# A delta-rule layer's last round with values ahead of queries, MLP weights over the masked operands, and the MLP norm's weight on the transposed input

## The chip, the cores and the metric

The kernel runs on one core of one Trainium2 chip. The metric is the device time of a run in microseconds (us); of several runs the median is given. Engines are named as in the profile: PE (TensorE matmuls), PEld (its weight loads), DVE (VectorE), ACT (ScalarE), POOL (GpSimd) and SP (SyncE, whose queue issues most of the DMAs). "L823" is line 823 of the kernel.

## The reference

The input is `x` (128 sequences of 32 tokens, 512 channels, fp32) and a context of 257 tokens per sequence. Three residual layers follow one another, each on a layer norm of `x`: a cross-attention, a delta-rule layer with its own SwiGLU MLP, and a Hadamard-rotated quantised feed-forward. The change lies in the second one:

```python
h = _rms(x, attn_norm_w)
q = silu(silu(_causal_dwconv(h @ Wq.T, conv_q)))     # 4 taps along the 32 tokens
k = silu(silu(_causal_dwconv(h @ Wk.T, conv_k)))
v = silu(silu(_causal_dwconv(h @ Wv.T, conv_v)))
q, k = _l2norm(q), _l2norm(k)                        # per head: 32 heads of 16
beta = jax.nn.sigmoid(h @ Wbeta.T)
o, memory_state = _delta_scan(k, q, v, beta)         # S -= beta * (S k - v) k^T ; o = S q
o = _rms(o, out_norm_w) @ Wout.T
x = x + o
h2 = _rms(x, mlp_norm_w)
x = x + silu(h2 @ Wgate.T) * (h2 @ Wup.T) @ Wdown.T  # 512 -> 1408 -> 512
```

The two norm weights `out_norm_w` and `mlp_norm_w` multiply channels, so they can be put on the rows of the weight matrices that read the normed tensor, or on the tensor itself.

## The kernel before

The program is written for a scheduler that keeps each engine's instructions in one fixed order and adds the semaphores; pools give the tiles their addresses, and a tile placed over the address of an earlier one waits for that one's last reader. Four stages follow each other: `cross_attention` (0 to about 697 us in the profile), `delta_products` (to about 1236), `delta_out_mlp` (to about 2413) and `hadamard_ffn` (to the end).

`delta_products` takes the 4096 tokens in 8 groups (rounds) of 512. A round has twelve channel steps: for each of four chunks of 128 channels a key step and a query step, k, q, k, q and so on, and then four value steps. A step is four 128x512 matmuls (L520, 3.44 us together), the convolution's taps and the activations. From keys and queries come two things: squared lengths (`add`, L577 to L581, then `lengths` and `by_tokens`), and, a block of 128 tokens at a time, the products of keys with keys and queries (`products`, L455 to L462), for which SP makes masked copies of `kq` (`kqm`, loaded at L550). The products go to DRAM as `ld` and `pd`. `put_v` (L618 to L627) transposes a finished value chunk on PE, scales it on DVE (L621, into `vt`) and stores it from POOL (L627, into `vd`). The reciprocal query lengths are stored by POOL too (L609, `rq`). In the last round the products of the last group are not made in the phase: keys and queries are stored as they are (`kd`, L666, on SP's queue), and `late_products` in the next phase makes them from there.

`delta_out_mlp` takes the tokens in 16 blocks of 256. For each block `back(b)` builds the outputs: it loads the solved `u` (L743), POOL spreads it into `um` (L750), SP loads `pe` (L757) from `pd`, PE multiplies them (L764), DVE makes `oT` (L777) with the lengths `r` (L773); then comes the output projection with `wo` (L797), the residual `y` (L800), the MLP norm's factor (L807, L808, L811), a transpose of each 128-token tile on PE (L97) and the copy of its result into `hT` (L812), one ACT instruction per tile. `mlp(b)` runs the gate (`wg`, L823) and up (`wu`, L826) matmuls on `hT`, silu on ACT (L828), the product `mT` on DVE (L829), the down projection (`wd`, L834) in two halves of 128 tokens, the residual add `xo` on DVE (L839), and then the next layer's statistics (L81, L82), `z` (L844) and butterflies (L126, L127). Beside it run `late_products` (masked loads `km`, L856, and `k`, L858) and the substitution solver, whose DVE steps (L432, L436, L442) get shorter from 31 x 64 to 1 x 64 elements per group of tokens. The function `mixed` interleaves these lists by given costs, and the last group's solve ends at about 2150 us.

At the border of the two phases the weights are loaded on SP's queue, in the trace in this order: `wo` and the first half of `wg` (L103), the MLP norm's weight `mnw` (L874), the first half of `wu`, the second halves, and after the first part of `back(0)` `wd`. DVE scales `wo` by the output norm, and ACT, at L888, `wg` and `wu` by `mnw` (sixteen instructions). In memory `wg` lies over masked operands and `wu` over masked operands and `kq`; the tile of `mnw` lies over `wv`.

Of the kernel before, what the change touches and what calls it, by code (L numbers as in the profile page):

```python
# [26 lines left out]
H = 32  # L27
HD = 16
TAPS = 4
SG = 512  # L30
EARLY = 24
FF = 1408
FC = FF // P
# [13 lines left out]
def pools(tc, *specs):  # L47


    stack = ExitStack()  # L50
    got = []
    for name, bufs, *space in specs:
        kw = {"space": space[0]} if space else {}
        got.append(stack.enter_context(tc.tile_pool(name=name, bufs=bufs, reuse_waits="tile", **kw)))
    return stack, got
# [44 lines left out]

def load_rows(nc, dst, src):

    nc.sync.dma_start(dst, src.rearrange("(c p) n -> p c n", p=P))  # L103


def mixed(*steps):


    lists = [[0.0, total, s] for total, s in steps if s is not None]
    while lists:  # L110
        one = min(lists, key=lambda a: a[0] / a[1])
        cost = next(one[2], None)
        if cost is None:
            lists.remove(one)
        else:
            one[0] += cost
# [268 lines left out]
NG = NT // SG  # L385
# [79 lines left out]
def delta_products(  # L465
# [8 lines left out]
    tc, nc = g.tc, g.nc  # L474
    KT = 256

    stack, (xp, wp1, hp, wk1, wp, st, wk, wp2, wk2, wp3, wk3, psn, psp, ps, psg) = pools(
        tc, ("b_x", 3), ("b_w1", 1), ("b_hn", 2), ("b_h", 2), ("b_w", 1), ("b_st", 2), ("b_k", 2),
        ("b_w2", 1), ("b_v", 2), ("b_m", 4), ("b_g", 6), ("b_pn", 1, PSUM), ("b_pp", 3, PSUM),
        ("b_ps", 2, PSUM), ("b_pg", 2, PSUM),  # L480
    )
    with stack:
        w, cw = {}, {}
        for n, src, p in (("k", wkT, wp1), ("q", wqT, wp1), ("v", wvT, wp2)):
            w[n] = p.tile([P, DC, D], FP, name=f"w{n}")
            load_rows(nc, w[n], src)
        w["b"] = wp.tile([P, DC, H], FP, name="wb")
# [7 lines left out]
        nc.sync.dma_start(cm, causal)  # L495
        scaled_rows(nc, wp, "nw", norm_w, [w["k"], w["q"], w["v"], w["b"]])

        kqm = [wp3.tile([P, HH, 2, KT], FP, name=f"kqm{i}", bufs=1) for i in range(3)]
        blank = [t[:, h] for t in kqm for h in range(HH)]
        mv, rs = stats  # L500

# [64 lines left out]
        class Group:  # L566
# [13 lines left out]
                nc.tensor.matmul(self.sums[H : 2 * H], w["b"][:, ec, :], hT[:, ec, :], **at)  # L580
                nc.tensor.matmul(self.sums[2 * H :], hs[:, ec, :], sq[:, 1], **at)  # L581

            def lengths(self):

                f = self.factors = wk.tile([3 * H, SG], FP, name="f", bufs=1)
                nc.scalar.activation(f[H : 2 * H], self.sums[H : 2 * H], AF.Tanh, scale=0.5)
                for r in (slice(0, H), slice(2 * H, 3 * H)):
                    nc.scalar.activation(f[r], self.sums[r], AF.Sqrt)

            def by_tokens(self):  # L590
                f = self.factors
                pt = ps.tile([P, GT, 2 * H], FP, name="ps")
                for i in range(GT):
                    nc.tensor.transpose(
                        pt[:, i, :], f[0 : 2 * H, i * P : (i + 1) * P], g.ident[0 : 2 * H, 0 : 2 * H]
                    )
                self.n = st.tile([P, GT, H], FP, name="n")
                nc.vector.tensor_scalar_max(self.n, pt[:, :, 0:H], 1e-12)
                self.beta = st.tile([P, GT, H], FP, name="beta")
                nc.vector.tensor_scalar(self.beta, pt[:, :, H:], 0.5, 0.5, ALU.mult, ALU.add)  # L600
                n2 = st.tile([P, GT, H], FP, name="n2", bufs=1)
                nc.vector.tensor_mul(n2, self.n, self.n)
                nc.vector.reciprocal(n2, n2)
                nc.vector.tensor_mul(self.beta, self.beta, n2)
                q = f[2 * H :]
                nc.vector.tensor_scalar_max(q, q, 1e-12)
                nc.vector.reciprocal(q, q)
                for c in range(DC):
                    nc.gpsimd.dma_start(  # L609
                        rq[self.gi, :, :, c].rearrange("i h t -> h i t"),  # L610
                        f[2 * H + c * HH : 2 * H + (c + 1) * HH].rearrange("h (i t) -> h i t", t=P),
                    )
# [25 lines left out]
        def a_round(gi, old, hT, made):  # L638
            new = Group(gi)
            made.append(new)  # L640
            xt, kq = [], {}
            if gi + 1 < NG:
                hT_next = wk1.tile([P, DC, SG], FP, name="hT")
                made.append(hT_next)
            for j, (n, ec) in enumerate(todo):
                if n == "v":
                    dst = new.v[ec] = wk2.tile([P, SG], FP, name="v2", bufs=4)
                else:
                    if n == "k":
                        kq[ec] = wp3.tile([P, 2, SG], FP, name="kq")  # L650
                    dst = kq[ec][:, "kq".index(n)]
                acc, last = channels(hT, n, ec)
                with tc.issue_after(last):
                    for _ in range(min(HH, len(blank))):
                        nc.vector.memset(blank.pop(0), 0.0)

                for _ in range(tiles[j]):
                    if count["done"] < per * len(held) and (old or j >= 4):
                        multiply()
                activated(acc, dst)  # L660
                if n == "q":
                    if gi < NG - 1:
                        pieces.extend((gi, ec, half, kq[ec]) for half in range(SG // KT))
                        hold()
                    else:
                        nc.sync.dma_start(kd[:, ec], kq[ec])  # L666
                if 3 <= j <= 9 and j % 2:
                    new.add(kq[(j - 3) // 2], hT, (j - 3) // 2)
                if j in loads and gi + 1 < NG:
                    xt.append(load((gi + 1) * GT + len(xt)))  # L670
                if j == 9:
                    new.lengths()
                    if gi == 0:
                        g.factors(*(t[:, EARLY:] for t in stats))
                if j == 11:
                    new.by_tokens()
                if j >= 8 and gi + 1 < NG:
                    normed((gi + 1) * GT + j - 8, xt[j - 8], hT_next)
                if old and j < DC:
                    old.put_v(j)  # L680
                yield 1
            if gi + 1 == NG:
                for ec in range(DC):
                    new.put_v(ec)

        hT = wk1.tile([P, DC, SG], FP, name="hT")
        for i in range(GT):
            normed(i, load(i), hT)
        old = None
        for gi in range(NG):  # L690
            made = []
            mixed((len(todo), a_round(gi, old, hT, made)), *beside(gi))
            old, hT = made[0], made[-1]
        assert count["done"] == per * len(pieces)


def delta_out_mlp(
# [14 lines left out]
    with stack:  # L712
# [4 lines left out]
        for t in (*um, *pe, km):  # L717
            nc.gpsimd.memset(t, 0.0)
        cm = lp.tile([P, T], FP, name="cm")
        wo = wp.tile([P, DC, D], FP, name="wo")  # L720
        wg = wp.tile([P, DC, FF], FP, name="wg")
        wu = wp.tile([P, DC, FF], FP, name="wu")
        wd = wp.tile([P, FC, D], FP, name="wd")
        inv_d = st.tile([P, 1], FP, name="inv_d", bufs=1)
        nc.vector.memset(inv_d, 1.0 / D)
        turn = {"pe": 0, "um": 0}
# [6 lines left out]
        def back(b):  # L733
# [75 lines left out]
            hT = wk2.tile([P, DC, TB], FP, name="hT")  # L809
            for i in range(NTL):  # L810
                nc.vector.tensor_scalar_mul(ys[i], ys[i], r[:, i : i + 1])  # L811
                nc.scalar.copy(hT[:, :, i * P : (i + 1) * P], g.transposed(ps, ys[i], g.ident))  # L812
                yield 2
            ready[b] = hT, xs

# [59 lines left out]

        for cols in (slice(0, 6 * P), slice(6 * P, FF)):
            for t, src in ((wg, wgT), (wu, wuT)):
                load_rows(nc, t[:, :, cols], src[:, cols])
        nc.sync.dma_start(cm, causal)
        mark = []  # L880
        first, late = back(0), late_products()
        mixed((4.0, part(first, 4.0)), (1.0, part(late, 1.0)))
        scaled_rows(nc, st, "onw", onorm_w, [wo])
        load_rows(nc, wd, wdT)
        for cols in (slice(0, 6 * P), slice(6 * P, FF)):
            for t in (wg, wu):
                for dc in range(DC):
                    nc.scalar.mul(t[:, dc, cols], t[:, dc, cols], nw[:, dc : dc + 1])  # L888
        mixed((12.0, first), (3.0, part(late, 3.0)))
        for b in range(NBL):  # L890
            mixed(
# [282 lines left out]
```

## Time and profile before

| what | value |
|---|---|
| time, median of 3 runs | 3081.3 us (3078.63 to 3082.94) |
| the profiled execution's own time | 3082.62 us |
| its span in the trace | 3080.8 us |
| mean granted PE clock | 0.986 |
| PE busy | 2924.4 us (95%) |
| PEld busy | 1678.8 us (54%) |
| DVE busy | 2077.8 us (67%) |
| ACT busy | 1040.3 us (34%) |
| POOL busy | 650.6 us (21%) |
| last value matmul of the last round ends | 1223.8 us |
| first gate matmul of the MLP | 1283.74 us |

Busy times come from the page's first part, the two moments from the timeline of PE. A row of the profile's groups reads: line, engine, operation, output<-input, number of instructions, then busy us, mean ns of one, and the idle time of the engine just before them with what ended it. A row of a timeline reads: start, us, engine, line, operation, count. In the page's rows of 40 digits each digit is one fortieth of the span (77 us).

### The profile page before, as it was taken

What the parts mean: (1) busy time and instruction counts of PE and PEld (TensorE: products, weight loads), DVE (VectorE), ACT (ScalarE), POOL (GpSimd) and SP (SyncE); (2) the same over time, 40 slices, a digit from 0 to 9 for tenths busy, and PEclk for the clock granted to TensorE, in tenths of its full rate; (3) what the DMA queues carried; (4) which work ended last, traced back from release to release, by engine and by line L of the source; (5) the groups of instructions that cost most, each with busy time, mean ns of one, the idle gap of its engine ahead of it and who ended that gap; (6) DMA issues with size and microseconds to landing.
All of it is one profiled execution on the core that took longest, in us unless ns stands there. A gap on an engine that the chain in (4) does not pass through costs nothing.

```text
span 3080.8 us, 42042 instructions
## 1 busy us (share of the span) xinstructions
PE 2924.4 (95%) x15558; PEld 1678.8 (54%) x15558; DVE 2077.8 (67%) x3557; ACT 1040.3 (34%) x1716; POOL 650.6 (21%) x963
## 2 busy tenths in 40 slices
PE   8999999999999999699999999999999899999998
PEld 3444443433333333467666766677777466666665
DVE  2353534336699797368778787878322599999997
ACT  1111111216666666212212121121111255555554
POOL 1121212113686664321211111001000000000000
PEclk9999999999999999799999999999999999999999
DMA  9798989763554544642322313131310111111110
GB/s 330 264 308 276 314 298 324 262 214 110 158 152 131 173 127 153 168 126 62 124 89 89 108 55 112 48 107 53 130 47 37 52 37 40 42 42 42 41 33 21
DMA packets 258235, 408.08 MB, mean 132 GB/s; under 512 B 68336, under 2 KB 170864, under 8 KB 254576
## 3 DMA queue, kind: packets, MB, share of 16 engines
q1 hardware_dynamic: 223856, 305.21, 31.8%
q0 software_dynamic: 34176, 100.19, 9.5%
q8 instruction: 124, 2.03, 0.3%
q14 instruction: 79, 0.65, 0.1%
HBM read 288.36 MB, written 93.85 MB: 124 GB/s over the span
## 4 chain that ended last, share of the span: by engine, by line
PE 37%; issue 24%; DVE 4%; DMA 2%; POOL 1%; ACT 0%; SPq 0%; POOLq 0%; DVEq 0%; ACTq 0%
PE pm L823 8%; PE pm L826 8%; PE pm L834 7%; PE pp L520 5%; PE ps L797 4%; PE pg L455 2%; PE ps L764 2%; DVE W L442 1%; DVE pr L436 1%; DMA xs<-x 1%; DMA wd<-in_WdownT_dram 1%; POOL out_dram L1030 1%; PE ps L97 1%; PE pm L455 0%; PE pn L579 0%
## 5 line engine op out<-in xcount | busy, mean ns | idle before, releaser
L823 PE MATMUL pm<-hT,wg 128*128 128x256 f32 x1408 | 341.4, 385 | 0.7 <-ACT hT L812 0.7
L826 PE MATMUL pm<-hT,wu 128*128 128x256 f32 x1408 | 333.9, 380 | 0.0
L436 DVE TENSOR_TENSOR pr<-L,W 128x1984 f32<-128x1984 f32 (+30 forms) x248 | 312.4, 1260 | 23.5 <-DMA L<-ld 19.6
L442 DVE TENSOR_TENSOR W<-W,pr 128x1984 f32<-128x1984 f32 (+30 forms) x248 | 309.6, 1249 | 3.2
L834 PE MATMUL pm<-wd,mT 128*128 128x512 f32 x704 | 307.2, 592 | 0.0
L823 PEld LDWEIGHTS pm<-hT,wg 128*128 128x128 f32 x1408 | 261.7, 190 | 57.3 <-issue 15.9
L826 PEld LDWEIGHTS pm<-hT,wu 128*128 128x128 f32 x1408 | 267.5, 190 | 36.2
L834 PEld LDWEIGHTS pm<-wd,mT 128*128 128x128 f32 x704 | 132.6, 190 | 160.8 <-issue 160.7
L828 ACT ACTIVATE sg<-pm 128x256 f32<-128x256 f32 x176 | 67.3, 383 | 348.3 <-PE pm L823 336.4
L829 DVE TENSOR_TENSOR mT<-pm,sg 128x256 f32<-128x256 f32 x176 | 73.9, 420 | 163.9 <-PE pm L826 151.5
L1030 POOL DMA_DIRECT2D out_dram<-xo x32 | 17.3, 542 | 638.2 <-DVE xo L1029 638.2
L992 ACT ACTIVATE s<-ps,f 128x512 f32<-128x512 f32 x128 | 85.5, 698 | 154.6 <-PE ps L987 154.6
L1027 PE MATMUL ps<-wq,q2T 128*128 128x512 bf16 x512 | 116.1, 380 | 21.9 <-ACT q2T L1024 21.9
L987 PE MATMUL ps<-wq,qT 128*128 128x512 bf16 x512 | 133.8, 385 | 2.1 <-ACT qT L974 2.1
L461 POOL TENSOR_TENSOR kk<-kk,cm 128x256 f32<-128x256 f32 x128 | 133.2, 1040 | 2.1
L990 PE MATMUL ps<-wq,qT 128*128 128x512 bf16 x512 | 133.0, 383 | 0.0
L951 ACT ACTIVATE t<-ps,magic,qs 128x512 f32<-128x512 f32 x160 | 114.0, 781 | 40.0 <-DVE qs L946 39.9
L458 POOL DMA_DIRECT2D ld<-kk x128 | 92.2, 720 | 149.2 <-ACT kk L457 141.9
L455 PE MATMUL pg<-kqm,kq 128*32 128x512 f32 x896 | 118.8, 601 | 4.2 <-DMA kqm<-kq 3.6
L346 PE MATMUL ps<-hT,wq 128*128 128x512 f32 x256 | 114.5, 606 | 7.2 <-ACT hT L339 7.2
L934 PE MATMUL ps<-hd,mT 128*128 128x128 f32 x1024 | 119.7, 275 | 0.3 <-ACT mT L1000 0.3
L302 PE MATMUL ps<-wo,aoT 128*128 128x512 f32 x256 | 117.0, 600 | 1.5 <-ACT aoT L295 1.5
(213 smaller groups left out, 5165.4 us busy)
## 6 DMA issues: line engine op xcount, KB each, us to landing
kall<-in_ctxT_dram SPq DMA_DIRECT2D x32, 2056.0 KB
cx<-in_ctx_dram SPq DMA_DIRECT2D x32, 2048.0 KB
x<-xo POOLq DMA_DIRECT2D x64, 256.0 KB, 3.5
xt<-x SPq DMA_DIRECT2D x64, 256.0 KB
ld<-kk POOLq DMA_DIRECT2D x128, 128.0 KB, 2.5
pd<-kk POOLq DMA_DIRECT2D x128, 128.0 KB, 2.3
L<-ld SPq DMA_DIRECT2D x8, 2048.0 KB
pe<-pd SPq DMA_DIRECT2D x256, 64.0 KB
```

The lines of the kernel that those rows point to most:

```text
L436: nc.vector.tensor_mul(pr[:, 0:n], bc(L[:, s, :, s + 1 : T].rearrange("p h t -> p t h"), HD), w[:, s].unsqueeze(1).to_broadcast([P, n, H4, ...
L442: nc.vector.tensor_sub(w[:, s + 1 :], w[:, s + 1 :], pr[:, 0:n])
L455: nc.tensor.matmul(pg[js], k[:, js], m[:, :, :, js], start=True, stop=True)
L461: nc.gpsimd.tensor_mul(kk[:, 1], kk[:, 1], cm.unsqueeze(1).to_broadcast([P, HH, T]))
L520: nc.tensor.matmul(pp.rearrange("p b t -> p (b t)"), w[n][:, dc, ec * P : (ec + 1) * P], hT[:, dc, :], start=dc == 0, stop=dc == DC - 1,)
L797: nc.tensor.matmul(pw, oT[:, i, dc, :], wo[:, dc, :], start=dc == 0, stop=dc == DC - 1)
L823: nc.tensor.matmul(pg, wg[:, dc, fs], hT[:, dc, :], start=dc == 0, stop=dc == DC - 1)
L826: nc.tensor.matmul(pu, wu[:, dc, fs], hT[:, dc, :], start=dc == 0, stop=dc == DC - 1)
L834: nc.tensor.matmul(pd, mT[:, fc, i * P : (i + 1) * P], wd[:, fc, :], start=fc == 0, stop=fc == FC - 1,)
L934: nc.tensor.matmul(pr[:, c * P : (c + 1) * P], xT[:, c0 + c, :], hd, start=True, stop=True)
L987: nc.tensor.matmul(pg, qT[:, dc, :], wg[:, dc, ks], start=dc == 0, stop=dc == DC - 1)
L990: nc.tensor.matmul(pu, qT[:, dc, :], wu[:, dc, ks], start=dc == 0, stop=dc == DC - 1)
```

## The change

It has three parts.

1. The last round is a function of its own, `last_round`. Its twelve steps go k, k, k, k, v, v, v, v, q, q, q, q. Key lengths and `by_tokens` come after the keys, query lengths (`put_q`) at the end; `put_v` of the round's own values stands at the query steps; the stores of `kd` go from SP's queue to ACT's.
2. Pools and tiles are placed anew. `kq` gets a pool of four buffers of its own below the masked operands, `wq` and `wv` change places, and in the MLP phase `wd` is allocated first, so that `wo`, `wg` and `wu` lie over the masked operands alone, `wd` over what lies below; the tile of `mnw` now lies over `wq`. The first part of `back(0)` is issued after the last of the weights' loads.
3. `wg` and `wu` are no longer scaled by `mnw`. Instead the transposed tile is multiplied by it on its way from PSUM into `hT`: four 128x128 multiplies per tile, by turns on ACT and DVE, where one 128x512 copy on ACT was.

```diff
-        for n, src, p in (("k", wkT, wp1), ("q", wqT, wp1), ("v", wvT, wp2)):
+        for n, src, p in (("k", wkT, wp1), ("q", wqT, wp2), ("v", wvT, wp1)):
...
+            def add_one(self, kq, hT, ec, of):
+                sq = wk.tile([P, 2, SG], FP, name="sq")
+                nc.scalar.activation(sq[:, 0], kq[:, "kq".index(of)], AF.Square)
+                at = dict(start=ec == 0, stop=ec == DC - 1)
+                rows = slice(0, H) if of == "k" else slice(2 * H, 3 * H)
+                nc.tensor.matmul(self.sums[rows], hs[:, ec, :], sq[:, 0], **at)
+                if of == "k":
+                    nc.tensor.matmul(self.sums[H : 2 * H], w["b"][:, ec, :], hT[:, ec, :], **at)
...
+        def last_round(gi, old, hT):
+            new = Group(gi)
+            kq = []
+            for j, (n, ec) in enumerate((n, ec) for n in "kvq" for ec in range(DC)):
...
+                acc, _ = channels(hT, n, ec)
+                for _ in range(2):
+                    if count["done"] < per * len(held):
+                        multiply()
+                activated(acc, dst)
+                if n == "q":
+                    nc.scalar.dma_start(kd[:, ec], kq[ec])
                     new.put_v(ec)
+                if j < DC:
+                    old.put_v(j)
+                if 1 <= j <= DC:
+                    new.add_one(kq[j - 1], hT, j - 1, "k")
+                elif j == DC + 1:
+                    new.lengths("k")
+                elif j == DC + 2:
+                    new.by_tokens()
+                elif n == "q" and ec:
+                    new.add_one(kq[ec - 1], hT, ec - 1, "q")
+                yield 1
+            new.add_one(kq[DC - 1], hT, DC - 1, "q")
+            new.lengths("q")
+            new.put_q()
...
+        wd = wp.tile([P, FC, D], FP, name="wd")
         wo = wp.tile([P, DC, D], FP, name="wo")
         wg = wp.tile([P, DC, FF], FP, name="wg")
         wu = wp.tile([P, DC, FF], FP, name="wu")
-        wd = wp.tile([P, FC, D], FP, name="wd")
...
-                nc.scalar.copy(hT[:, :, i * P : (i + 1) * P], g.transposed(ps, ys[i], g.ident))
+                pt = g.transposed(ps, ys[i], g.ident)
+                for dc in range(DC):
+                    (nc.vector.tensor_scalar_mul if dc % 2 else nc.scalar.mul)(
+                        hT[:, dc, i * P : (i + 1) * P], pt[:, dc, :], nw[:, dc : dc + 1]
+                    )
...
-        mixed((4.0, part(first, 4.0)), (1.0, part(late, 1.0)))
+        with tc.issue_after(weights.ins):
+            mixed((4.0, part(first, 4.0)), (1.0, part(late, 1.0)))
         scaled_rows(nc, st, "onw", onorm_w, [wo])
         load_rows(nc, wd, wdT)
-        for cols in (slice(0, 6 * P), slice(6 * P, FF)):
-            for t in (wg, wu):
-                for dc in range(DC):
-                    nc.scalar.mul(t[:, dc, cols], t[:, dc, cols], nw[:, dc : dc + 1])
```

The chunks of `hT` are called dc0 to dc3 below.

More of the change, by code (lines that the diff above doesn't have):

```diff
@@ L101, in load_rows @@
 def load_rows(nc, dst, src):
-    nc.sync.dma_start(dst, src.rearrange("(c p) n -> p c n", p=P))
+    return nc.sync.dma_start(dst, src.rearrange("(c p) n -> p c n", p=P))
 def mixed(*steps):
@@ L475, in delta_products @@
     KT = 256
-    stack, (xp, wp1, hp, wk1, wp, st, wk, wp2, wk2, wp3, wk3, psn, psp, ps, psg) = pools(
+    stack, (xp, wp1, hp, wk1, wp, st, wk, wp2, kqp, wk2, wp3, wk3, psn, psp, ps, psg) = pools(
         tc, ("b_x", 3), ("b_w1", 1), ("b_hn", 2), ("b_h", 2), ("b_w", 1), ("b_st", 2), ("b_k", 2),
-        ("b_w2", 1), ("b_v", 2), ("b_m", 4), ("b_g", 6), ("b_pn", 1, PSUM), ("b_pp", 3, PSUM),
+        ("b_w2", 1), ("b_kq", 4), ("b_v", 2), ("b_m", 1), ("b_g", 6), ("b_pn", 1, PSUM), ("b_pp", 3, PSUM),
         ("b_ps", 2, PSUM), ("b_pg", 2, PSUM),
@@ L496, in delta_products @@
         scaled_rows(nc, wp, "nw", norm_w, [w["k"], w["q"], w["v"], w["b"]])
-        kqm = [wp3.tile([P, HH, 2, KT], FP, name=f"kqm{i}", bufs=1) for i in range(3)]
+        kqm = [wp3.tile([P, HH, 2, KT], FP, name=f"kqm{i}") for i in range(3)]
         blank = [t[:, h] for t in kqm for h in range(HH)]
@@ L581, in add, with lengths @@
                 nc.tensor.matmul(self.sums[2 * H :], hs[:, ec, :], sq[:, 1], **at)
[L583 to L588, printed above, removed]
+            def add_one(self, kq, hT, ec, of):
[6 more added lines that the diff above has]
+                    nc.tensor.matmul(self.sums[H : 2 * H], w["b"][:, ec, :], hT[:, ec, :], **at)
+            def lengths(self, of="kq"):
+                if "k" in of:
+                    f = self.factors = wk.tile([3 * H, SG], FP, name="f", bufs=1)
+                    nc.scalar.activation(f[H : 2 * H], self.sums[H : 2 * H], AF.Tanh, scale=0.5)
+                for n, r in (("k", slice(0, H)), ("q", slice(2 * H, 3 * H))):
+                    if n in of:
+                        nc.scalar.activation(self.factors[r], self.sums[r], AF.Sqrt)
             def by_tokens(self):
@@ L604, in by_tokens, with put_q @@
                 nc.vector.tensor_mul(self.beta, self.beta, n2)
+            def put_q(self):
+                f = self.factors
                 q = f[2 * H :]
@@ L641, in a_round @@
             xt, kq = [], {}
-            if gi + 1 < NG:
-                hT_next = wk1.tile([P, DC, SG], FP, name="hT")
-                made.append(hT_next)
+            hT_next = wk1.tile([P, DC, SG], FP, name="hT")
+            made.append(hT_next)
             for j, (n, ec) in enumerate(todo):
@@ L649, in a_round @@
                     if n == "k":
-                        kq[ec] = wp3.tile([P, 2, SG], FP, name="kq")
+                        kq[ec] = kqp.tile([P, 2, SG], FP, name="kq")
                     dst = kq[ec][:, "kq".index(n)]
@@ L661, in a_round @@
                 if n == "q":
[L662 to L666, printed above, removed]
+                    pieces.extend((gi, ec, half, kq[ec]) for half in range(SG // KT))
+                    hold()
                 if 3 <= j <= 9 and j % 2:
                     new.add(kq[(j - 3) // 2], hT, (j - 3) // 2)
-                if j in loads and gi + 1 < NG:
+                if j in loads:
                     xt.append(load((gi + 1) * GT + len(xt)))
@@ L676, in a_round @@
                     new.by_tokens()
-                if j >= 8 and gi + 1 < NG:
+                    new.put_q()
+                if j >= 8:
                     normed((gi + 1) * GT + j - 8, xt[j - 8], hT_next)
@@ L681, in a_round @@
                 yield 1
-            if gi + 1 == NG:
-                for ec in range(DC):
-                    new.put_v(ec)
+        def last_round(gi, old, hT):
+            new = Group(gi)
+            kq = []
+            for j, (n, ec) in enumerate((n, ec) for n in "kvq" for ec in range(DC)):
+                if n == "k":
+                    kq.append(kqp.tile([P, 2, SG], FP, name="kq"))
+                if n == "v":
+                    dst = new.v[ec] = wk2.tile([P, SG], FP, name="v2", bufs=4)
+                else:
+                    dst = kq[ec][:, "kq".index(n)]
+                acc, _ = channels(hT, n, ec)
[5 more added lines that the diff above has]
+                    nc.scalar.dma_start(kd[:, ec], kq[ec])
+                    new.put_v(ec)
+                if j < DC:
[11 more added lines that the diff above has]
+            new.lengths("q")
+            new.put_q()
         hT = wk1.tile([P, DC, SG], FP, name="hT")
@@ L689, in delta_products @@
         old = None
-        for gi in range(NG):
+        for gi in range(NG - 1):
             made = []
             mixed((len(todo), a_round(gi, old, hT, made)), *beside(gi))
-            old, hT = made[0], made[-1]
+            old, hT = made
+        mixed((len(todo), last_round(NG - 1, old, hT)), *beside(NG - 1))
         assert count["done"] == per * len(pieces)
@@ L877, in delta_out_mlp @@
             for t, src in ((wg, wgT), (wu, wuT)):
-                load_rows(nc, t[:, :, cols], src[:, cols])
+                weights = load_rows(nc, t[:, :, cols], src[:, cols])
         nc.sync.dma_start(cm, causal)
```

## The prediction

> **What bounds the kernel now.** I read the page's 40 slices first, then the costliest groups, then the chain and the waits of the only stretch where TensorE is not full.
>
> ```profile
> PE   8999999999999999699999999999999899999998
> DVE  2353534336699797368778787878322599999997
> PEclk9999999999999999799999999999999999999999
> ...
> L823 PE MATMUL pm<-hT,wg 128*128 128x256 f32 x1408 | 341.4, 385 | 0.7 <-ACT hT L812 0.7
> ```
>
> Each digit is 77 us. TensorE (PE) is full in all phases except one slice, the seventeenth (1232 to 1309 us), where it is busy to six tenths at a lower clock: the seam between the delta rule's last round and the first MLP block. The last row is the gate matmul of the MLP: in 16 blocks it waited 0.7 us altogether for hT, the transposed input that this change writes differently. From the first gate matmul (1283.7) on, PE has no slack to lose into: between 1295 and 2325 us its waits sum to 5.8 us. VectorE (DVE) is busy to seven or eight tenths up to about 2150 us, in twelve blocks, because the substitution solver (L432, L436, L442) stands in its queue.
>
> The seam in windows (columns: length, busy us of PE, PEld, DVE, ACT, POOL, granted clock, DMA share, GB/s):
>
> ```profile
> 1215.00:1225.00 10.00, 9.75 (x32) 3.85 (x30) 3.98 (x9) 9.11 (x11) 0.00 (x0) 1.00 0.75 272
> 1225.00:1235.00 10.00, 1.63 (x9) 1.34 (x10) 9.64 (x13) 9.32 (x15) 2.85 (x7) 0.62 0.99 351
> 1235.00:1245.00 10.00, 0.96 (x5) 0.56 (x3) 0.00 (x0) 7.46 (x11) 2.81 (x4) 0.50 1.12 261
> 1245.00:1255.00 10.00, 3.64 (x64) 2.84 (x64) 2.47 (x5) 0.00 (x0) 6.16 (x9) 0.52 1.03 308
> ```
>
> From 1225 to 1255 the sixteen DMA engines are full (share about 1) while PE does 6 us of work: the seam is a matter of transfers. SyncE's queue at its start, and what PE waits for:
>
> ```profile
> 1214.63 0.51 SPq L103 DMA_DIRECT2D wg<-in_WgateT_dram  x1
> 1223.81 0.37 SPq L874 DMA_DIRECT2D mnw<-in_mlp_norm_dram  x1
> 1224.28 0.44 SPq L103 DMA_DIRECT2D wu<-in_WupT_dram  x1
> ...
> 1225.92 1.86 SPq L743 DMA_DIRECT2D u<-ud  x1
> ```
>
> ```profile
> PE ps L764 <- POOL um L750: 14.7, 1, 14.7
> ```
>
> wo and half of wg are issued at 1214; then the queue stands 9 us at the small norm load mnw, whose tile lies over a weight of the delta phase and so waits for the last value matmul. um comes at 1250.2, although u landed at 1239.4, because POOL is held by the value stores (vd) in front of it. oT follows at 1254.4, the second tile's at 1270.2, the first gate matmul at 1283.7.
>
> [...] um left POOL 10.8 us after its data, right behind the vd stores. [...] Prices: [...] the trace's nearest row, beta<-ps 128x128, has 0.280, which I use. [...] no row of before has this form, its 128x768 scalings took 0.92 [...].
>
> **The change part by part.**
>
> *Rounds 0 to 6 and the start of the phase.* The instructions keep their order on each engine. wq and wv change places in memory: wq is now the late load. It is ready at 704.4 by the times of before's late one, and the first query matmul stood at 704.6: cost 0, at most 0.5 us, hidden by the four key matmuls.
>
> *Weights over the masked operands.* wg and wu now lie where only the masked copies were, free some steps into the last round. But the mnw load is still first in SyncE's queue, and its tile now lies over wq, whose last reader is the last query matmul, which the new order puts at the very end. wo, wg, wu and u are queued behind it. Last-round PE work from 1169.8 on: 12 channels x 3.44, five products 4.85, seven transposes x 0.59, length sums 4 x 0.96 + 1.0 and 0.4 of rest, sum 55.4, so the end is 1225.2. So the 6.8 MB of wo, wg and wu start at 1225.7, none of it early. Before's halves of 1.31 MB landed 3.4 us apart (385 GB/s): 17.9 us, with 1.2 to start 1244.8; 1.0 MB of kd stores now on ScalarE's queue and up to 1.1 MB of vd stores share the engines: up to 5 us more. u follows at 1246 to 1251 (before 1239.4), but POOL's vd stores are earlier now and no longer hold um. The pe loads reuse semaphores of the weight loads, the last lands about 2.2 us after u. First oT 1252.5 to 1256.5 (before 1254.4). The wd load (2.9 MB, about 8 us) goes out behind it at some 1256, not at 1240.5, and the second tile's loads queue behind wd: second oT 1269 to 1273 (before 1270.2). With about 1 us for the new hT chain the first gate matmul comes at 1281 to 1287: **seam -3 to +4, taken +1.5**.
>
> *Queues that the last round is moved across.* The four kd stores (0.34 us each to issue on SyncE's row) go out on ScalarE between channels of 3.4 us of PE work, hidden. The query lengths now end the round: on DVE their reciprocal (L607, 3.34 us a time), on POOL the four rq stores (L609, 2.2 us), in front of um. Both are over by about 1236, ten us ahead of u: 0; if u landed at once they would cost 2.2.
>
> *Sixteen scalings of wg and wu on ScalarE* (4 each of 0.92, 0.93, 0.81, 0.81: 13.9 us between 1227 and 1242.5) go. ScalarE then idled 12.7 us for oT, so 0.
>
> *hT.* Where one copy of 0.586 us on ScalarE stood per 128-row tile (32 of them) there are four 128x128 multiplies, ScalarE, VectorE, ScalarE, VectorE, and by the tile's dependences each waits for the one ahead: a chain of four handovers through two in-order queues. In DVE's queue stands the solver. The block boundary at 1434, before:
>
> ```profile
> 1434.05 0.68 DVE L839 TENSOR_TENSOR xo<-pm,xs 128x512 f32<-128x512 f32 x1
> 1434.65 1.22 DVE L442 TENSOR_TENSOR W<-W,pr 128x1024 f32<-128x1024 f32 x1
> 1435.78 0.69 DVE L81 BATCH_NORM_STATS2 bn_st<-xo 128x6 f32<-128x512 f32 x1
> 1436.38 0.21 DVE L432 TENSOR_TENSOR W<-W 128x64 f32<-128x64 f32 x1
> 1436.51 0.18 DVE L82 BATCH_NORM_AGGREGATE mvx<-bn_st 128x2 f32<-128x6 f32 x1
> 1436.62 1.16 DVE L436 TENSOR_TENSOR pr<-L,W 128x960 f32<-128x960 f32 x1
> 1437.70 0.48 DVE L844 TENSOR_SCALAR z<-xo,mvx 128x512 f32<-128x512 f32 x1
> ```
>
> Here PE's transposes began at 1433.60 and ScalarE's copy was done at 1434.83. In the changed program dc1 stands after L82 and dc3 after z, another solver step and the first butterfly pair. This stretch is already as long as PE's half block: 10.1 us of DVE against 9.9 of PE. Two multiplies of the first tile and a shifted solver step make the residual add about 0.6 later: 1434.7. Start to start 0.61, 1.14, 0.60, 0.13, 0.12 lead to dc1 at 1437.3, done 1437.65. PE meanwhile has five L764-type matmuls, the dc0 pair (2 x 0.43, from 1434.7), 27 more at 0.056 and one product of 0.3: at 1437.3 it waits 0.3. The dc1 and dc2 matmuls (4 x 0.43) take it to 1439.4; DVE reaches dc3 after 0.20, 0.40, 1.07, 0.34, 0.34, at 1439.65, done 1440.0: 0.6 more. About 1 us lost in this block. The same sum for the other solver blocks gives 0.14 to 1.07 us, **7.6 us for the twelve**; where 1984-wide steps (2.1 us) stand, products and the next gate's first matmuls cover most of it. The last three boundaries, without solver, give 0: dc3 is done 2.3 us after the residual add, and the 27 matmuls cover it. The extra VectorE work is 64 x 0.28 = 18 us, in a queue with 46 of 65 us taken per block: 0 on the path elsewhere.
>
> Sum: 7.6 + 1.5 = **+9 us** on the profiled execution's 3082.6, which stands 1.3 above the median of 3081.3; so about 3091 for a median. PE work itself changes by nothing, and the Hadamard phase stays.
>
> Bounds. hT below: nothing lost, if the handovers fall into the fill: 0. Above: 1 us more of DVE lag in each of the twelve, as the residual add's own lag reached 1.85 in one block before: 7.6 + 12 = 20. Seam below -8, if um comes as early as POOL allows and takes the second tile along; above +8, if wd and the second tile's loads collide.
>
> **Rivals.**
> - *hT chain through the busy DVE* (likeliest): +3 to +20 with the seam's ±4, 3085 to 3105.
> - *Hidden*: the fill covers the handovers and the seam moves nothing, 3077 to 3087. For it: PE has 1.5 to 2 us of other matmuls after dc0. Against: DVE's stretch is full already.
> - *Seam wins (faster)*: POOL freed from the vd stores starts um when u lands. If u lands before 1244, first and second tile move up 6 to 10 us, and the sum is 3070 to 3076. It decides from a seam shortened by more than the hT loss, about 14 us for 6 net at my sizes, or 8 if hT costs 2. For it: 14.7 us of PE wait name um, and the removed scalings crowded ScalarE there. Against: mnw still holds the weights back, and u is behind them.
> - *The DVE lag accumulates*: solver steps held back push mT and PE's buffers, +25 to +35, 3106 to 3116. Against: 19 us of slack per block.
>
> **How the numbers follow.** Chances: hT chain 0.48, hidden 0.24, seam wins 0.20, lag accumulates 0.08. A run can tell 0.2% (6 us). Of the hidden case most is within that, of the hT case a part below +6: faster 0.23, same 0.23, slower 0.54. The prediction is 3091, the likeliest's; the range 3073 to 3109 takes the hidden case whole, half of the seam's gain and half of the accumulation out. The likeliest alone: 3085 to 3105.
>
> **What would show it.** Right: the mnw load issued at about 1225 with wo behind it; 64 VectorE rows for hT at 0.28; PE waits at the gate matmul naming DVE hT, some 0.5 us per block in 1295 to 2100 and none after 2200; first gate matmul 1281 to 1287. Wrong: wo before 1215, a first gate matmul before 1278, PE waits on hT under 2 us or above 15 in total.

## The result and the profile after

The changed kernel takes 3097.2 us (median of 6 runs, 3090.7 to 3104.1), the kernel before, run beside it, 3082.1: ratio 1.0042, 95% interval 1.0027 to 1.0056, so slower by 0.27 to 0.56%. (Ratios here and below are not quotients of the two medians; that quotient would be 1.0049.) The forecast was 3091, slower, and the time lies in its range. But the two terms of its sum are the wrong way round. Taken apart between the two profiled executions (spans 3080.8 and 3095.4), with the moments from PE's timeline ("channel matmul" is L520; a stretch that begins with the last one begins at its end):

| stretch | before | after | difference | forecast |
|---|---|---|---|---|
| start to first channel matmul of `delta_products` | 701.1 | 702.0 | +0.9 | 0 |
| rounds 0 to 6 | 469.6 | 470.3 | +0.7 | 0 |
| last round, first to last channel matmul | 53.1 | 56.1 | +3.0 | in the seam |
| last channel matmul to first gate matmul | 60.0 | 71.3 | **+11.3** | seam +1.5 |
| first gate matmul to last down matmul | 1129.0 | 1127.2 | **-1.8** | hT +7.6 |
| Hadamard phase | 668.1 | 668.5 | +0.5 | 0 |

The loss is in the seam and the round ahead of it; the MLP blocks, where the forecast put most of it, are no slower. The page, its slices and the gate group after:

```profile
PE   8999999999999999499999999999999899999998
PEclk9999999999999999699999999999999999999999
...
L872 PE MATMUL pm<-hT,wg 128*128 128x256 f32 x1408 | 347.6, 386 | 0.5 <-ACT hT L859 0.5
```

The seventeenth slice has gone from six tenths to four, at a lower clock (digit 6, before 7); all others of PE's row are as they were. The gate matmuls wait for hT 0.5 us in total. Now the queue and who waited. First SyncE's longest wait over 1200 to 1300 us (waited for: us in total, times, longest), then rows of its timeline, then PE's two longest waits in the same stretch:

```profile
SPq L923 <- PE pp L520: 57.9, 1, 57.9
```

```profile
1228.46 0.39 SPq L923 DMA_DIRECT2D mnw<-in_mlp_norm_dram  x1
...
1229.67 0.37 SPq L103 DMA_DIRECT2D wo<-in_WoutT_dram  x1
1230.08 0.50 SPq L103 DMA_DIRECT2D wg<-in_WgateT_dram  x1
...
1247.27 0.70 SPq L788 DMA_DIRECT2D u<-ud  x1
...
1265.49 0.40 SPq L103 DMA_DIRECT2D wd<-in_WdownT_dram  x1
```

```profile
PE ps L809 <- POOL um L795: 23.0, 1, 23.0
PE ps L809 <- DMA pe<-pd: 10.2, 1, 10.2
```

SyncE stands 57.9 us at the mnw load, until the last query matmul, with every weight behind it. wo, the first half of wg and the rest, of which before had 2.6 MB on their way from 1214, are all issued from 1229.7 on; u follows them and lands at 1259.4 (1239.4 before). Then wd goes out between the two 128-token tiles of the first block, and the second tile's pe comes behind it. In the kernel before, wd was issued at 1240.5, ahead of the first tile's matmuls. PE's rows, first before, then after: the last channel matmul, the matmuls with pe of the first and the second tile, the first gate matmul.

```profile
1221.47 2.31 PE L520 MATMUL pp<-hT,wv 128*128 128x512 f32 x5
...
1250.66 3.64 PE L764 MATMUL ps<-pe,um 128*32 128x128 f32 x64 [14.69 <-POOL um L750]
...
1262.46 1.93 PE L764 MATMUL ps<-pe,um 128*32 128x128 f32 x32 [0.85 <-DMA pe<-pd]
...
1283.74 2.78 PE L823 MATMUL pm<-hT,wg 128*128 128x256 f32 x8
```

```profile
1227.84 0.59 PE L520 MATMUL pp<-hT,wq 128*128 128x512 f32 x1
...
1260.27 3.64 PE L809 MATMUL ps<-pe,um 128*32 128x128 f32 x64 [23.04 <-POOL um L795]
...
1279.41 1.93 PE L809 MATMUL ps<-pe,um 128*32 128x128 f32 x32 [10.20 <-DMA pe<-pd]
...
1299.72 0.48 PE L872 MATMUL pm<-hT,wg 128*128 128x256 f32 x1
```

From the end of the last channel to the first tile it is 31.8 us (26.9 before), from the first tile to the second 19.1 (11.8 before), from there to the gate 20.3 (21.3 before): +5.0, +7.3 and -1.0 make the 11.3.

The windows show that the DMA engines were not full at the start of the seam (DMA share and GB/s are the last two columns; before had 0.99 and 351 in its first such window):

```profile
1230.00:1240.00 10.00, 2.96 (x4) 0.32 (x4) 4.83 (x6) 4.39 (x6) 1.50 (x2) 0.73 0.84 233
1240.00:1250.00 10.00, 0.00 (x0) 0.00 (x0) 3.36 (x5) 0.00 (x0) 3.97 (x5) 0.50 1.01 375
1250.00:1260.00 10.00, 0.00 (x0) 0.00 (x0) 0.00 (x0) 0.00 (x0) 0.59 (x2) 0.50 0.93 289
```

### The profile page after: what moved, and what is told of

It is laid out like the page before. It is cut to its first block, busy times and chain, and to the rows that moved or that the text cites. A ratio compares the mean times of both kernels' runs of the same rounds, so it can differ in the third digit from the quotient of the medians.

```text
span 3095.4 us, 42105 instructions
## 1 busy us (share of the span) xinstructions
PE 2932.8 (95%) x15558; PEld 1675.7 (54%) x15558; DVE 2091.6 (68%) x3621; ACT 1029.6 (33%) x1734; POOL 653.0 (21%) x963
## 4 chain that ended last, share of the span: by engine, by line
PE 62%; ACT 3%; DVE 1%; DMA 1%; issue 1%; SPq 0%; POOL 0%; POOLq 0%; DVEq 0%; ACTq 0%
PE pm L872 10%; PE pm L883 10%; PE pm L875 10%; PE pp L520 5%; PE ps L980 4%; PE ps L842 4%; PE ps L1033 4%; PE ps L1073 3%; PE ps L1036 3%; PE ps L97 3%; PE ps L809 2%; PE pg L455 2%; ACT q2T L1070 1%; PE pm L455 1%; ACT qT L1020 1%
## 5 line engine op out<-in xcount | busy, mean ns | idle before, releaser
L872 PE MATMUL pm<-hT,wg 128*128 128x256 f32 x1408 | 347.6, 386 | 0.5 <-ACT hT L859 0.5
L436 DVE TENSOR_TENSOR pr<-L,W 128x1984 f32<-128x1984 f32 (+30 forms) x248 | 312.3, 1259 | 23.5 <-DMA L<-ld 19.1
L1073 PE MATMUL ps<-wq,q2T 128*128 128x512 bf16 x512 | 116.1, 380 | 21.9 <-ACT q2T L1070 21.9
L455 PE MATMUL pg<-kqm,kq 128*32 128x512 f32 x896 | 119.0, 601 | 4.2 <-DMA kqm<-kq 3.6
L520 PE MATMUL pp<-hT,wk 128*128 128x512 f32 x256 | 119.5, 607 | 0.6 <-DVE acc L527 0.4
```

What stands on the lines that cost most here:

```text
L436: nc.vector.tensor_mul(pr[:, 0:n], bc(L[:, s, :, s + 1 : T].rearrange("p h t -> p t h"), HD), w[:, s].unsqueeze(1).to_broadcast([P, n, H4, ...
L455: nc.tensor.matmul(pg[js], k[:, js], m[:, :, :, js], start=True, stop=True)
L520: nc.tensor.matmul(pp.rearrange("p b t -> p (b t)"), w[n][:, dc, ec * P : (ec + 1) * P], hT[:, dc, :], start=dc == 0, stop=dc == DC - 1,)
L872: nc.tensor.matmul(pg, wg[:, dc, fs], hT[:, dc, :], start=dc == 0, stop=dc == DC - 1)
L1073: nc.tensor.matmul(pd, qT[:, c, :], wd[:, c, :], start=c == 0, stop=c == IC - 1)
```

## The experiments

Two theories. The **queue theory**: the seam is set by where loads stand in SyncE's queue and what the loads ahead of them wait for. The **hT theory**, the prediction's: the four-step multiply loses time at every block boundary. Rivals inside the queue theory are bandwidth (kd and vd stores take time of the same 16 engines as the weights whenever they go: in the changed kernel, from 1225 to 1262 us, the loads took 65.8% of it, the kd stores 13.4% and POOL's stores 6.2%) and the round's order itself. Ratios are to the kernel before, run beside it on the same chip; "seam" is last channel matmul to first gate matmul of the profiled execution (60.0 before, 71.3 changed). Whole profiled executions compare badly: the first channel matmul of the delta phase comes between 700.9 and 713.2 us in the thirteen of them, behind a stage that no edit touches. So stretches are compared. Parts 1 and 3 of the change were run alone; part 2, the places in memory, was not.

**Norm loads behind the weights** (in the changed kernel):

```diff
-        nc.sync.dma_start(nw, norm_w.rearrange("(c p) -> p c", p=P))
...
         with tc.issue_after(weights.ins):
             mixed((4.0, part(first, 4.0)), (1.0, part(late, 1.0)))
-        scaled_rows(nc, st, "onw", onorm_w, [wo])
+            nc.sync.dma_start(nw, norm_w.rearrange("(c p) -> p c", p=P))
+            scaled_rows(nc, st, "onw", onorm_w, [wo])
```

> The changed kernel with the two small norm loads (mnw, onw) issued behind the weights' loads. Queue theory: the 16 us that the first gate matmul comes later (1299.7 against 1283.7) come from the weights' loads standing behind mnw, which waits for the last query matmul. Then wo goes out at about 1190 (its own wait is the last masked product), u lands near 1235, um comes at about 1244 (POOL still holds it behind the zeroing of km and the rq stores), the first gate matmul at about 1280, and the run takes about 3078 (-19 on 3097). hT theory (the prediction's): the loss is in the blocks, so 3093 to 3097. Bandwidth theory: kd and vd stores crowd the engines at the end of the round whenever the weights go, so -5 at most.

3087.9 us, ratio 1.0008 (0.9994 to 1.0023): of the loss of 0.42% nearly all is gone, and the two intervals do not meet. The seam is 54.2, 17 less than in the changed kernel. But the last round takes 60.4 instead of 56.1, which is part of why the forecast of 3078 was missed.

**wd behind the second tile** (in the changed kernel):

```diff
-        load_rows(nc, wd, wdT)
         mixed((12.0, first), (3.0, part(late, 3.0)))
+        load_rows(nc, wd, wdT)
```

> The changed kernel with the load of wd moved behind the second tile's loads. From the first oT to the second tile's matmuls it is 19.1 us in the changed kernel and 11.8 before; queue theory: the 2.9 MB of wd stand between the first and second tile's u and pe. Then the second tile's loads land near 1270 instead of 1280, the first gate matmul at about 1291, the run takes about 3089 (-8). hT theory: no change, 3097. Should wd come too late for the first down matmul, a new wait shows at L883 and the gain is lost.

3091.7 us, ratio 1.0027 (1.0019 to 1.0035). First to second tile 11.3 us (19.1 changed, 11.8 before), seam 63.0, 8.3 less than changed. The time alone would not show it, since the interval overlaps that of the changed kernel. No wait for wd shows at the down matmuls.

**Both.**

> Both: norm loads behind the weights, wd behind the second tile's loads. Queue theory: gains add for the most part, first gate matmul about 1272, 3070 (-27), faster than both kernels. If the two waits cover each other: 3078, as with the norm loads alone. hT theory: 3093 to 3097.

3082.9 us, ratio 0.9998 (0.9986 to 1.0011): the seam is 47.5, so the two gains add there (17.1 and 8.3 alone, 23.8 together), while the last round has again lost 4.4 us (60.5). The forecast 3070 was missed by that and by what stands next in the queue. SyncE in this kernel:

```profile
1186.19 0.39 SPq L103 DMA_DIRECT2D wo<-in_WoutT_dram  x1
...
1224.20 0.37 SPq L103 DMA_DIRECT2D wu<-in_WupT_dram  x1
1238.92 0.34 SPq L927 DMA_DIRECT2D cm<-in_causal_dram  x1
1239.36 0.38 SPq L788 DMA_DIRECT2D u<-ud  x1
```

wo is 43 us earlier, but the second half of wu waits until 1224 and cm until 1239, the moments at which the first and the last kd store have landed. For wu the reason is a semaphore, whose number each DMA in the trace names and whose updates there mark its landing: the second half of wu and the first kd store have the same one, of a set that the DMAs of SyncE's and of ScalarE's queue take in turn. (In the changed kernel's trace the set has eight. There it is the first half of wu that shares with the first kd store, and that one had landed at 1223.62, 7.3 us before wu went out.) cm waits for the last kd store by another semaphore than its own. On POOL the zeroing of km, which is allocated just ahead of cm, waits for the same landing, so both probably lie over memory that kd is stored from; that was not tested. And um stands right behind this zeroing and the rq stores:

```profile
1239.06 1.80 POOL L763 MEMSET km<- 128x2048 f32 x1 [5.68 <-DMA kd<-kq]
1242.56 2.21 POOL L624 DMA_DIRECT2D rq<-f  x4 [1.69 <-DVE f L622]
1244.76 0.76 POOL L795 COPY um<-u 128x256 f32<-128x256 f32 x2
```

**hT copied again** (the changed kernel with one copy per tile and the sixteen scalings back):

```diff
-                for dc in range(DC):
-                    (nc.vector.tensor_scalar_mul if dc % 2 else nc.scalar.mul)(
-                        hT[:, dc, i * P : (i + 1) * P], pt[:, dc, :], nw[:, dc : dc + 1]
-                    )
+                nc.scalar.copy(hT[:, :, i * P : (i + 1) * P], pt)
```

> The changed kernel with hT as before: one copy per tile on ScalarE, and wg and wu scaled by mnw on ScalarE after they land. hT theory (the prediction's): -7.6 us, 3089. Hidden theory: the blocks' pitch in the changed kernel (1127.2 us from first gate to last down, 1129.0 before) says that the chain costs nothing on the whole; 3097 within 3, or slower by up to 5 where the sixteen scalings now come after the late weights and ahead of the first silu.

3093.5 us, ratio 1.0035 (1.0024 to 1.0047), overlapping the changed kernel's interval. First gate to last down is 1125.7 against 1127.2: 1.4 us less, not 7.6.

**hT alone** (the same edit the other way round, in the kernel before, and the scalings taken out).

> The kernel before with the hT part of the change alone (four multiplies per tile, wg and wu not scaled). The changed kernel with hT copied stood 3.7 us under the changed one (3093.5 against 3097.2, in different calls). hT theory: +3 to +8 on before. Hidden theory: within 2 of before; the sixteen scalings on ScalarE that go stood in front of the last values' activations (v, L535), so a part of the seam may come back: down to -4.

3081.6 us, ratio 1.0008 (0.9999 to 1.0016). First gate to last down 1127.9, against 1129.0 before; the seam, without the sixteen scalings, is 57.7, 2.3 less. So in neither setting does hT cost what was forecast. Over all profiled executions this stretch takes 1126.1 to 1128.5 us in the ten with the new hT and 1125.7 to 1129.0 in the three with the old. Why the cost is nearly nothing, the waits of PE in the blocks show: before (1295 to 2325 us) they are

```profile
PE pm L783 <- DVE sq L782: 3.2, 4, 1.1
PE pm L783 <- DVE W L432: 2.6, 2, 2.3
```

and with hT alone no wait of PE is left in that stretch. With hT copied in the changed kernel the two are back (5.4 us). Summing PE's steps from one start to the next by kind, the products (L455), behind which PE now meets dc1, take 16.1 us instead of 13.3 with the new hT, in both settings: 2.8 us that the chain costs, hidden from the list of waits. The gate and up matmuls, whose steps take in the waits at L783, take 3.2 us less in this setting and 4.6 in the other. Cost and gain cancel. That the gain comes from a shift of DVE's queue, so that sq is there when L783 wants it, is an inference from the two waits going, not tested by itself.

**The order of the last round alone** (part 1 of the change in the kernel before, with that kernel's pools and hT).

> The kernel before with the last round's order alone (values ahead of queries, kd on ScalarE's queue; pools, places of wq and wv, and hT as before). Here mnw lies over wv, so it is released by the last value matmul, near 1212, and the issue order on SyncE is mnw, u and most of pe, then wo and the rest behind the last query's work. Queue theory: the seam is set by where the loads stand in SyncE's queue, not by the order of the channels; u and pe land early, um is held by POOL's km and rq to about 1245, the weights land near 1255: first gate matmul near 1280, time 3080 (-3), with +3 us for the round itself included. Order theory (the round's new order is itself what costs): the last round 56.1 instead of 53.1 us and the query lengths on the path: +8 or more, 3091.

3094.1 us (4 runs), ratio 1.0049 (1.0032 to 1.0066): as slow as the changed kernel. In its profiled execution the round takes 3.0 us and the seam 5.5 us more than before (65.5), 8.5 together where the changed kernel has 14.3; another 8.1 us lie ahead of the delta phase, so the size of this loss is less certain than its sign. The expectation had set queue against order as if only one could be; the order alone costs, and in the trace it costs through the queue. u is issued early indeed. But then the second tile's xs holds the queue for 12.8 us, until the last query matmul, and pe waits 7.8 us for POOL to zero its tile, behind vd stores:

```profile
1219.39 0.45 SPq L788 DMA_DIRECT2D u<-ud  x1
...
1241.89 2.52 SPq L802 DMA_DIRECT2D pe<-pd  x3
1244.46 0.42 SPq L103 DMA_DIRECT2D wo<-in_WoutT_dram  x1
...
1250.51 7.24 SPq L802 DMA_DIRECT2D pe<-pd  x5
```

Three of the eight pe loads come ahead of the weights and five behind them, landing at 1267; PE waits 23.8 us for them. The round itself takes 56.1 instead of 53.1. By PE's steps, 1.8 of this is work that stood behind the last channel before, twelve transposes of the round's own values (1.5 us) and those of `by_tokens` (0.3); that is not lost. The length sums take 1.1 us more (5.0 instead of 3.9), since those of the queries no longer run beside those of the keys: in the kernel before three of the small matmuls at a time start within 0.02 us of each other; in the changed kernel the two of a query chunk take 1.0 us by themselves.

**wq and wv back in their old places** (one line of the changed kernel):

```diff
-        for n, src, p in (("k", wkT, wp1), ("q", wqT, wp2), ("v", wvT, wp1)):
+        for n, src, p in (("k", wkT, wp1), ("q", wqT, wp1), ("v", wvT, wp2)):
```

> The changed kernel with wq and wv in their old places, so that mnw lies over wv again and waits for the last value matmul (about 1212) instead of the last query matmul (1228). Queue theory: wo goes out at 1212, u lands near 1243, um at 1246 behind POOL's rq, wd still between the tiles, first gate matmul near 1285: 3086 (-11). If it is not mnw but the later waits in the queue (cm, kd's landing) that count: 3094.

3087.9 us, ratio 1.0034 (1.0020 to 1.0048). The seam is 58.8, 12.5 less than in the changed kernel, about what was forecast for the gate. The time does not show it: with five runs its interval overlaps that of the changed kernel. The second half of wu and cm wait for kd here too.

**kd back on SyncE's queue** (one word of the changed kernel: `nc.sync` for `nc.scalar`).

> The changed kernel with the kd stores back on SyncE's queue. The weights then stand behind the last kd store, so wo goes out at about 1234.5 instead of 1229.7. Queue theory: what counts is when the weights' loads start, +4.8: 3102. Bandwidth theory: from 1229 to 1257 the engines carry a fixed number of bytes, kd and vd stores among them, so the end of the weights is the same: 3097.

3097.3 us (4 runs), ratio 1.0044 (1.0027 to 1.0060), wide enough for both forecasts; the trace is with the bandwidth theory. wo goes out 5.1 us behind the last channel instead of 1.2, and lands in 6.6 us instead of 11.4; the last weight lands 27.1 us behind the last channel instead of 29.0. The seam is 67.6 (71.3 changed), the round 57.3 (56.1). In the changed kernel the start that is 3.9 us earlier is worth nothing: wo's load takes 4.8 us more beside the kd stores.

**A version to beat both**, in three steps. First: norm loads and wd behind as above, cm behind the first tile's loads, kd on POOL's queue, the first block's um copied by ScalarE.

```diff
-                    nc.scalar.dma_start(kd[:, ec], kq[ec])
+                    nc.gpsimd.dma_start(kd[:, ec], kq[ec])
...
-                    nc.gpsimd.tensor_copy(m[:, :, e, e * HD : (e + 1) * HD], uv[:, :, e, 0:HD])
+                    (nc.gpsimd.tensor_copy if b else nc.scalar.copy)(
+                        m[:, :, e, e * HD : (e + 1) * HD], uv[:, :, e, 0:HD]
+                    )
```

> A version to beat both: norm loads behind the weights, wd behind the second tile, cm behind the first tile's loads, the first block's um copied by ScalarE instead of POOL, kd stored by POOL instead of ScalarE (whose DMAs share their landing semaphores with SyncE's). Queue theory: u and pe land about 1236, um at 1240 (behind ScalarE's square root of the query lengths), second tile about 1251, first gate matmul about 1270, 6 less than with the norm loads and wd alone: 3076 (-7 on before). If the second tile's loads then wait for kd's landing and km: no better than 3082.

3077.3 us, ratio 0.9989 (0.9979 to 0.9999). u lands at 1219.9, ahead of the round's end, and the seam is 43.2; the last round now takes 61.8. What each of the edits brings by itself was not measured. Second: the norm loads behind the first tile's loads, and the second tile's loads ahead of the late products'.

```diff
-            mixed((4.0, part(first, 4.0)), (1.0, part(late, 1.0)))
+            mixed((4.0, part(first, 4.0)))
+            nc.sync.dma_start(nw, norm_w.rearrange("(c p) -> p c", p=P))
+            scaled_rows(nc, st, "onw", onorm_w, [wo])
+            mixed((4.0, part(first, 4.0)))
+            mixed((1.0, part(late, 1.0)))
             nc.sync.dma_start(cm, causal)
```

> As e9_seam_freed, with the norm loads behind the first tile's loads and the second tile's loads ahead of the late products' km and k (which wait for kd's landing). Queue theory: in e9 the second tile's u is issued at 1250 behind km, k, cm and the norms; now it goes at about 1237 and the pe quarters as the first tile's matmuls release them, so the second tile starts near 1249 instead of 1255 and the gate near 1269 instead of 1277: 3070 to 3072 (-10 on before). If the late products' k is what PE waits for next: 3076, as e9.

3077.8 us, ratio 0.9989 (0.9977 to 1.0001): no gain on the first step, the case that the expectation named last. First to second tile takes 6.8 us instead of 12.7, but the gate comes 44.9 after the last channel, not sooner: the late products' k is what PE waits for now (5.3 us in two waits). Third: `bufs=4` for vt.

> As e10_tiles_first, with four buffers for vt instead of two. In the runs with early weights the last round takes 60.4 to 61.8 us instead of 56.1, and PE waits 2.7 for a squared key; contention theory: the weights' transfers slow the vd stores, vt's two buffers stay taken, DVE and so the convolution of the last keys stand. Then the round comes back to 57 or less, and the run is 4 under e10: 3067. If the round stays at 60 or more, it isn't vt.

3073.4 us (5 runs), ratio 0.9958 (0.9934 to 0.9982): faster than both kernels, 4.3 us under the second step where 4 were forecast, though the intervals of these two just overlap. The round takes 57.3 instead of 62.0, as forecast, and this is what shows the cause. DVE's longest wait at vt from 1180 to 1240 us, with two buffers and then with four:

```profile
DVE vt L636 <- DMA vd<-vt: 7.1, 2, 6.4
```

```profile
DVE vt L636 <- PE ps L633: 7.8, 6, 3.0
```

With two buffers DVE stands 7.1 us for vd stores to land, beside the weights' transfers, and 4.4 us for PE's transposes; with four the first wait does not occur and the second is 7.8.

## Why the prediction was right or wrong

- *Time and sign*: right. **The reason given for them was wrong**, and the time was met by luck, because two misses of opposite sign nearly cancelled (seam +14.3 for +1.5 if the round is counted with it, hT -1.8 for +7.6). One of the prediction's own signs of being wrong came: PE's waits on hT were to be above 2 us, and the gate matmuls waited 0.5. The first gate matmul came at 1299.7, not at 1281 to 1287. (The sum as written, +9 on a median of 3081.3, is 3090, not 3091.)
- *mnw first in the queue, over wq, held by the last query matmul*: right, 57.9 us of wait at that one load. The last channel ended at 1228.4, not at 1225.2: the round began 1.6 later and its work was summed 1.6 short.
- *The seam's transfers*: the term that failed most. From wo's issue to the last weight's landing it was put at 19.1 us, at 385 GB/s, and up to 24.1 with the kd and vd stores; it took 27.7. The rate of the halves once under way was right (1.31 MB in 3.2 and 3.6 us), but it did not hold from the start: the first 11.4 us brought wo and little else of the weights, with two kd stores and some vd beside it, at 230 GB/s, and the rest went at 373. With kd on SyncE and mostly ahead of the weights, the same stretch took 21.9. Why the rate is low while the stores run beside the load is not shown.
- *u at 1246 to 1251, first oT at 1252.5 to 1256.5, second at 1269 to 1273*: measured 1259.4, 1264.4 and 1285.3. That wd stands between the tiles was seen, but from oT to oT it was given 16.5 us (15.8 before), and it took 20.8; the run with wd behind has a seam shorter by 8.3.
- *POOL*: that the vd stores would no longer hold um was right. That km and rq are over by 1236 was wrong (1247.4, since zeroing km waits for kd's landing at 1243.3); it cost nothing here, u being later still, and it set um in the version with both loads moved.
- *hT*: the mechanism was there, the size was not. At the boundary that was worked out, after:

```profile
1447.71 0.69 DVE L81 BATCH_NORM_STATS2 bn_st<-xo 128x6 f32<-128x512 f32 x1
...
1448.53 0.32 DVE L859 TENSOR_SCALAR hT<-ps,mnw 128x128 f32<-128x128 f32 x1
...
1450.90 0.34 DVE L859 TENSOR_SCALAR hT<-ps,mnw 128x128 f32<-128x128 f32 x1
```

  PE's transposes began at 1445.07. dc1 was done 3.8 us later (forecast 4.05) and dc3 6.2 later (6.4), while PE's next matmuls on dc1 began 4.5 later and those on dc3 6.3: the dc0 pair, the 27 small matmuls and a second product took about 0.7 us more than summed, so DVE was ready first. A wait of 1 us was the small difference of two sums of four to six, each good to about half a microsecond. And only a loss was priced: that DVE's shifted queue could remove a wait that the profile showed (5.8 us at L783) was not asked. A smaller slip: the 46 of 65 us that VectorE was said to be busy per block is the mean over all sixteen; in windows of the kernel before that hold solver steps from end to end it is 48 to 56.
- *Rivals*: "hidden" had hT right, covered by PE's other matmuls, but took the seam to stand still. "seam wins" had the right place with the wrong sign. Its mechanism became true in the versions with the loads rearranged: u landing ahead of the round's end, seam 43 us.

## What to carry to other kernels

A load of two kilobytes at the head of an in-order queue can hold seven megabytes (here mnw, where the queue stood 57.9 us with 6.8 MB of weights behind it): before placing large tiles over early-freed memory, look where the *small* tiles of the same queue lie, and what their last reader is. A load that is moved earlier can slow the stores that run there (in the kernel before, vd stores issued from 1213 to 1262 us, beside the weights, landed in 7.8 us, over the whole run in 3.6): give them another buffer first (vt here, 4.3 us). When a sum holds two terms of opposite uncertainty, check each with its own run; a total that comes out right does not confirm either.

## What was not expected of the hardware

DMAs issued from ScalarE's queue delayed SyncE's by their landings: with the norm loads moved, the second half of wu went out at 1224.20 just as kd's first store landed (1224.18), and cm, with u behind it, at 1238.92 as its last did (1238.84). For wu the trace shows the cause, one set of semaphores (eight in the changed kernel) that the DMAs of both queues take in turn; for cm it is probably its place in memory. Loads with stores from another queue beside them moved 230 GB/s in the changed kernel's first 11.4 us, and 373 after that. A 128x128 multiply from PSUM took 0.335 us on average on VectorE, where the nearest row of before, with constants for operands, had 0.280; on ScalarE it took 0.368.
